# Expert-choice routing behind a GRU: the search for each expert's last weight, by 17 bits and MAX8 instead of 30 bits and a stage for ties

## The chip, the core and the metric

The kernel runs on one core of a Trainium2 chip. The metric is device time in microseconds; before the change the median of three runs is 1204.65 us (1203.07 to 1211.93). A profile of one execution stands beside it. The names of the engines in it: PE is TensorE (PEld its weight loads), DVE VectorE, ACT ScalarE, POOL GpSimd, SP SyncE, which issues most of the transfers.

## What is computed

A GRU runs over 256 steps for 16 sequences of width 512. Its states are 4096 tokens. A router gives each token a softmax over 16 experts, and every expert chooses the k = 256 tokens that have the largest weights for it (expert choice). All experts share one matrix, so a token's result is its expert output times the sum of the weights with which it was chosen.

```python
def cell(h, x):                       # scanned over 256 steps
    gi = x @ W_ih + b_ih
    gh = h @ W_hh + b_hh
    r = sigmoid(i_r + h_r); z = sigmoid(i_z + h_z)
    n = tanh(i_n + r * h_n)
    return (1.0 - z) * n + z * h

logits = xf @ router_w + router_b     # xf: the 4096 states
S = softmax(logits, axis=-1)
G, idx = top_k(S.T, 256)              # each of 16 experts takes 256 tokens
out = einsum('ekh,hd->ekd', xf[idx], expert_w) + expert_b
y = zeros.at[idx].add(G[..., None] * out)
return x + y
```

Top-k takes the earlier token where weights are equal. So a kernel that finds the k-th largest weight of each expert, and keeps all weights at or above it, agrees with the reference as long as exactly 256 weights are kept; where several weights equal the k-th, it also has to rank them.

## The kernel before

The 256 steps are cut into 32 groups of 8 steps; a group is 128 tokens (16 sequences x 8 steps) and fills the partitions. The recurrence (all lines up to 538) takes most of the time and is the same in both kernels. Between its steps TensorE also makes the expert product of the states for 15 of the groups. The other 17 are "late groups" (line 124: the odd ones and the last but one): their expert product is made after the recurrence, by a generator that is called wherever TensorE would stand idle. `late_part` (line 132) is the smallest piece of it, a part: four matmuls with 256 columns each, side by side in four column strips. Eight parts are a group, so there are 136 parts. `expert_for(n)` (line 181) emits the next n parts at this place of TensorE's order.

A late group is summed in a PSUM bank. There are five banks for it (`ps_m` two, `ps_e` three). `late_begin` (line 153) writes the bias into a bank with ScalarE; it is emitted in the middle of the group two before it and has to wait until the bank's former content is used. As long as the gates are not known, a finished group is copied to SBUF by ScalarE (line 175). Once they are known (`gated`), it stays in its bank and the last step reads it there (line 172).

The routing stage (lines 566 to 678) has TensorE, ScalarE and VectorE in the order in which the code is written. The 4096 weights of an expert are laid out as 8 partitions of 512 elements (`sT`, by four transposes). A positive float32 orders like its bit pattern, so the k-th largest weight is found bit by bit, from bit 29 down to 0 (line 599): VectorE compares all weights with a candidate and counts per partition (line 602), TensorE adds the counts of an expert's eight partitions with the 0/1 matrix `same_h` (line 607), and two tiny VectorE steps (610 and 613) keep or drop the bit. Behind each count's matmul stand two late parts, or three where the bit is odd (line 608). The result `kth` is exact.

Then comes the stage for equal weights (lines 623 to 657): where a weight equals `kth`, its rank among its equals is found by a scan in a partition and two matmuls across partitions (641, 642), and compared with the room that is left below 256 (648 to 652). Ten late parts stand beside it. Kept weights are multiplied out in four pieces (660), each followed by a matmul (663) that sums a token's weights over the experts into `pg`. That becomes `gate` (665).

In the last step (670 to 678) VectorE makes for each group `xs = sums * gate + xs` (673) and SyncE stores the group, 256 KB each (676). The 15 groups of the recurrence come first, then the late groups as they finish: TensorE's remaining parts are emitted one by one in line 672 until the next late group is done.

Of the kernel before, what the change touches and what calls it, by code (L numbers as in the profile page):

```python
# [8 lines left out]
F32 = mybir.dt.float32  # L9
BF16 = mybir.dt.bfloat16  # L10
F16 = mybir.dt.float16
I32 = mybir.dt.int32
AF = mybir.ActivationFunctionType
ALU = mybir.AluOpType
AX = mybir.AxisListType
# [3 lines left out]
def kernel(  # L19
# [34 lines left out]
    nc = tc.nc  # L54
    B, T, D = x.shape
    E = router_w.shape[1]
    P = 128
    QD = 32
    KC = D // P
    TG = P // B  # L60
    NG = T // TG
    TOPK = min(B * T // E, B * T)
# [3 lines left out]
    xs = const.tile([P, NG, D], F32, name="xs")  # L66
# [4 lines left out]
    lg = const.tile([P, E, NG], F32, name="lg")  # L71
    eb = const.tile([P, D], F32, name="eb")
# [4 lines left out]
    QG = NG * E // P  # L77
    GH = P // E
# [31 lines left out]
    def begin_sums(bank):  # L110

        n = bank.shape[-1]
        for j in range(KC):
            nc.tensor.matmul(
                bank[QD * j : QD * (j + 1)],
                zero,
                zero[:, 0:E].unsqueeze(1).to_broadcast([P, n // E, E]),
                start=True,
                stop=True,
                tile_position=(0, QD * j),  # L120
            )
# [4 lines left out]
    def wide(g):  # L126

        return ht[:, g, :, :].rearrange("p k d -> p (k d)")
# [3 lines left out]
    def late_part(g, pe, part):  # L132

        k, h = divmod(part, 2)
        cols = slice(HD * h, HD * (h + 1))
        for j in range(KC):
            q = slice(QD * j, QD * (j + 1))
            nc.tensor.matmul(  # L138
                pe[q, cols],
                ht[:, g, k, q],  # L140
                ewr[:, k, E:][:, cols],
                start=False,
                stop=(k == KC - 1),
                tile_position=(0, QD * j),
                skip_group_check=True,
            )

    late = []
    late_sums = {}
# [31 lines left out]
    def expert_for(n):  # L181
        for _ in range(n):
            next(parts, None)
# [382 lines left out]
    with (  # L566
        tc.tile_pool(name="route", bufs=1) as rt,
        tc.tile_pool(name="work", bufs=2) as wk,
        tc.tile_pool(name="ps_s", bufs=1, space=bass.MemoryType.PSUM) as ps_s,
        tc.tile_pool(name="ps_c", bufs=1, space=bass.MemoryType.PSUM) as ps_c,  # L570
        tc.tile_pool(name="ps_n", bufs=1, space=bass.MemoryType.PSUM) as ps_n,
        tc.tile_pool(name="ps_e", bufs=3, space=bass.MemoryType.PSUM) as ps_e,
        tc.manual_schedule(engines={mybir.EngineType.PE, mybir.EngineType.Activation, mybir.EngineType.DVE}),
    ):
        late_pool.append(ps_e)
        keep = rt.tile([P, B, QG * TG], F32, name="keep")
        nc.gpsimd.memset(keep, 1.0)
        nc.gpsimd.memset(keep[:, :, 0:1], 0.0)

        ps = ps_s.tile([P, QG, P], F32, name="ps", tag="s")  # L580
        ps_last = ps_n.tile([P, P], F32, name="ps_last", tag="n")
        lg_f = lg.rearrange("p e g -> p (e g)")
        sT = rt.tile([P, QG * P], F32, name="sT")
        for q in range(QG - 1):
            nc.tensor.transpose(ps[:, q, :], lg_f[:, q :: QG], ident)
        nc.tensor.transpose(ps_last, lg_f[:, QG - 1 :: QG], ident)
        by_row = lambda ap: ap.rearrange("p (q b t) -> p b q t", q=QG, b=B)
        by_step = lambda ap: ap.rearrange("p b (q t) -> p b q t", q=QG)
        nc.scalar.copy(sT[:, 0 : (QG - 1) * P], ps[:, 0 : QG - 1, :].rearrange("p q n -> p (q n)"))
        nc.vector.tensor_copy(sT[:, (QG - 1) * P :], ps_last)  # L590

        HIGH = 29
        cand = wk.tile([P, 1], I32, name="cand")
        nc.vector.memset(cand, 1 << HIGH)
        ge = rt.tile([P, QG * P], BF16, name="ge")
        counts = ps_c.tile([P, HIGH + 1], F32, name="counts")
        for bit in range(HIGH, -1, -1):
            cnt = wk.tile([P, 1], F16, name="cnt")  # L600
            with nc.allow_low_precision("whole numbers up to a row's length, exact in float16"):
                nc.vector.tensor_scalar(
                    ge, sT, cand.bitcast(F32), None, ALU.is_ge, ALU.add, accum_out=cnt
                )

            n = counts[:, bit : bit + 1]
            nc.tensor.matmul(n, same_h, cnt, start=True, stop=True)
            expert_for(2 + bit % 2)
            off = wk.tile([P, 1], I32, name="off")
            nc.vector.tensor_scalar(off, n, float(TOPK), float(1 << bit), ALU.is_lt, ALU.mult)  # L610
            nxt = wk.tile([P, 1], I32, name="cand")
            if bit:
                nc.vector.scalar_tensor_tensor(
                    nxt, cand, 1 << (bit - 1), off, ALU.bitwise_or, ALU.bitwise_xor
                )
            else:
                nc.vector.tensor_tensor(nxt, cand, off, ALU.bitwise_xor)
            cand = nxt
        kth = cand.bitcast(F32)

        eq = rt.tile([P, B, QG * TG], F32, name="eq")
        nc.vector.tensor_scalar(by_step(eq), by_row(sT), kth, None, ALU.is_equal)
        rank = rt.tile([P, B, QG * TG], F32, name="rank")
        nc.vector.tensor_tensor_scan(
            rank.rearrange("p b t -> p (b t)"),
            keep.rearrange("p b t -> p (b t)"),
            eq.rearrange("p b t -> p (b t)"),
            0.0,  # L630
            ALU.mult,
            ALU.add,
        )
        row = rt.tile([P, B], F32, name="row")
        nc.vector.tensor_scalar(row, rank[:, :, QG * TG - 1], -1.0, None, ALU.mult)
        upto = rt.tile([P, B], F32, name="upto")
        nc.vector.tensor_tensor_scan(upto, ones_b, row, 0.0, ALU.mult, ALU.add)
        nc.vector.tensor_tensor(upto, upto, row, ALU.subtract)
        expert_for(4)
        n_first = ps_n.tile([P, B], F32, name="n_first", tag="n")  # L640
        nc.tensor.matmul(n_first, before_f, row, start=True, stop=False)
        nc.tensor.matmul(n_first, same_f, upto, start=False, stop=True)
        expert_for(6)
        at_least = rt.tile([P, QG * P], F32, name="at_least")
        nc.vector.scalar_tensor_tensor(at_least, sT, kth, sT, ALU.is_ge, ALU.mult)
        nc.vector.tensor_tensor(rank, rank, eq, ALU.mult)
        too_few = rt.tile([P, HIGH + 1], F32, name="too_few")
        nc.vector.tensor_copy(too_few, counts)
        nc.vector.scalar_tensor_tensor(too_few, too_few, float(TOPK), too_few, ALU.is_lt, ALU.mult)
        room = rt.tile([P, 1], F32, name="room")  # L650
        nc.vector.tensor_reduce(room, too_few, AX.X, ALU.max)
        nc.vector.tensor_scalar(room, room, -1.0, float(TOPK), ALU.mult, ALU.add)
        last = rt.tile([P, B], F32, name="last")
        nc.vector.tensor_scalar(last, n_first, room, 0.0, ALU.add, ALU.max)
        nc.vector.tensor_tensor(
            rank, rank, last.unsqueeze(2).to_broadcast([P, B, QG * TG]), ALU.is_le
        )
        pg = ps_s.tile([P, QG, GH], F32, name="pg", tag="s")
        for q in range(QG):
            nc.vector.tensor_tensor(  # L660
                by_row(at_least)[:, :, q, :], by_step(rank)[:, :, q, :], by_row(at_least)[:, :, q, :], ALU.mult
            )
            nc.tensor.matmul(pg[:, q, :], at_least[:, q * P : (q + 1) * P], row_of, start=True, stop=True)
        gate = rt.tile([P, NG], F32, name="gate")
        nc.vector.tensor_copy(
            gate.rearrange("p (h q) -> p h q", q=QG), pg.rearrange("p q h -> p h q")
        )

        gated.append(True)
        for g in [g for g in range(NG) if g not in late_groups] + late_groups:  # L670
            while g in late_groups and g not in late_done:
                expert_for(1)
            nc.vector.scalar_tensor_tensor(  # L673
                xs[:, g, :], late_sums.get(g, wide(g)), gate[:, g : g + 1], xs[:, g, :], ALU.mult, ALU.add
            )
            nc.sync.dma_start(
                out=out[:, g * TG : (g + 1) * TG, :], in_=xs[:, g, :]
            )


# [29 lines left out]
```

## Time and profile before

| | us |
|---|---|
| median of three runs | 1204.65 (1203.07 to 1211.93) |
| the profiled execution: its time | 1206.33 |
| the profiled execution: its span, first to last instruction | 1204.3 |
| TensorE busy | 1162.3 (97%) |
| TensorE weight loads busy | 1048.4 (87%) |
| VectorE busy | 699.2 (58%) |
| ScalarE busy | 323.3 (27%) |
| mean granted TensorE clock | 0.995 |
| first transpose of the routing stage ends, about | 1120 |
| first compare of the search | 1120.77 |
| the last candidate, line 617 | 1166.61 |
| first add of the last step | 1174.03 |
| last add starts | 1198.15 |

The span is the time between the first and the last instruction of the profiled execution; 2.0 us of that execution's time lie around it. A row of instructions in order of time gives start, duration, engine, line, operation, output and inputs, shapes and how many were merged; in brackets stands how long the engine was idle before it and what ended that wait. A matmul in float32 leaves two records for each instruction. Where a row says "issue", the profile shows nothing that the engine waited for.

### The profile page before, as it was taken

Reading aid. Unit: us, or ns where it says so; the run is one execution under the profiler, and the core shown is the slowest. Engines: PE = TensorE matmul, PEld = TensorE weight load, DVE = VectorE, ACT = ScalarE, POOL = GpSimd, SP = SyncE. Lnnn points to the kernel's source line nnn. Section 1 sums busy time; section 2 is a strip of 40 time slices with the busy share of each in tenths; the row PEclk is TensorE's granted clock in tenths of the full one; section 3 lists DMA queues with packets and bytes.
Section 4 is the critical chain, followed back from the end, with each engine's and each line's share of the span. In section 5 each row is a group of like instructions: output and inputs, shape, how many; then the busy total and the mean of one; then the engine's idle time right before and its main releaser. Section 6 shows DMA issues by size and latency. Waiting matters only on the chain. (4 is left out here: it accounts for less than half of the span.)

```text
span 1204.3 us, 80850 instructions
## 1 busy us (share of the span) xinstructions
PE 1162.3 (97%) x36490; PEld 1048.4 (87%) x36490; DVE 699.2 (58%) x3919; ACT 323.3 (27%) x1435; POOL 100.2 (8%) x406
## 2 busy tenths in 40 slices
PE   5999999999999999999999999999999999999897
PEld 3899999999999988999999999999889999998444
DVE  2555655565555555555565556565555555565777
ACT  0223222222222222222222222222222222222220
POOL 3000000000000000000000000000000000000000
PEclk9999999999999999999999999999999999999998
DMA  8000000000000000000000000000000000000008
GB/s 273 23 22 20 20 20 20 19 20 20 20 22 20 20 18 19 20 19 20 22 19 20 17 22 20 20 20 20 19 20 20 20 20 20 22 9 13 2 2 280
DMA packets 48345, 38.05 MB, mean 32 GB/s; under 512 B 7744, under 2 KB 40064, under 8 KB 48000
## 3 DMA queue, kind: packets, MB, share of 16 engines
q1 hardware_dynamic: 45856, 29.43, 8.4%
q8 instruction: 286, 4.69, 1.6%
q10 hardware_dynamic: 1632, 3.15, 0.8%
q14 instruction: 59, 0.48, 0.1%
q0 software_dynamic: 512, 0.31, 0.1%
HBM read 24.47 MB, written 8.39 MB: 27 GB/s over the span
## 5 line engine op out<-in xcount | busy, mean ns | idle before, releaser
L411 PE MATMUL ra<-whh,hs 128*16 128x128 f32 (+1 forms) x8192 | 345.6, 273 | 7.6 <-DVE zT L497 5.2
L411 PE MATMUL hn<-whh,hs 128*16 128x128 f32 (+1 forms) x8192 | 345.4, 273 | 0.0
L485 DVE TENSOR_TENSOR t<-r,hn 128x64 f32<-128x64 f32 x512 | 90.2, 217 | 364.1 <-PE hn L411 360.6
L398 PE MATMUL ra<-wih,xt 128*32 128x256 f32 x4096 | 288.0, 382 | 7.6 <-DVE xt L253 6.0
L411 PE MATMUL zz<-whh,hs 128*16 128x128 f32 (+1 forms) x8192 | 287.8, 273 | 2.6 <-issue 2.4
L411 PEld LDWEIGHTS ra<-whh,hs 128*16 128x16 f32 (+1 forms) x8192 | 243.3, 103 | 16.8 <-issue 6.8
L411 PEld LDWEIGHTS hn<-whh,hs 128*16 128x16 f32 (+1 forms) x8192 | 256.8, 103 | 0.4 <-issue 0.2
L411 PEld LDWEIGHTS zz<-whh,hs 128*16 128x16 f32 (+1 forms) x8192 | 239.6, 103 | 6.2 <-issue 5.5
L468 ACT ACTIVATE r<-ra 128x128 f32<-128x128 f32 x256 | 71.1, 278 | 598.4 <-PE ra L411 598.4
L398 PEld LDWEIGHTS ra<-wih,xt 128*32 128x32 f32 x4096 | 156.6, 111 | 43.2 <-issue 8.3
L489 ACT ACTIVATE n<-t 128x64 f32<-128x64 f32 x512 | 103.4, 248 | 192.8 <-DVE t L487 192.5
L398 PE MATMUL zz<-wih,xt 128*32 128x128 f32 x4096 | 147.1, 273 | 1.5 <-issue 1.2
L398 PEld LDWEIGHTS zz<-wih,xt 128*32 128x32 f32 x4096 | 128.9, 110 | 17.2 <-issue 4.1
L494 DVE STREAM_TRANSPOSE nT<-n 128x64 f32<-128x64 f32 x512 | 100.6, 234 | 57.3 <-ACT n L489 57.0
L497 DVE STREAM_TRANSPOSE zT<-zs 128x64 f32<-128x64 f32 x512 | 121.8, 238 | 3.7 <-ACT zs L490 3.1
L508 DVE TENSOR_TENSOR hs<-v,nT 128x32 f32<-128x32 f32 x512 | 101.7, 199 | 21.7
L505 DVE TENSOR_TENSOR v<-u,zT 128x32 f32<-128x32 f32 x512 | 104.3, 204 | 8.8
L365 PE MATMUL pe<-ewr,ht 128*32 128x136 f32 (+1 forms) x1920 | 107.6, 276 | 0.0
L487 DVE TENSOR_TENSOR t<-t,ra 128x64 f32<-128x64 f32 x512 | 88.2, 213 | 0.1
L365 PEld LDWEIGHTS pe<-ewr,ht 128*32 128x32 f32 x1920 | 75.0, 110 | 11.8 <-issue 0.2
L500 DVE TENSOR_TENSOR u<-hs,nT 128x32 f32<-128x32 f32 x512 | 78.2, 153 | 0.0
L138 PE MATMUL pe<-ewr,ht 128*32 128x256 f32 x1088 | 69.4, 395 | 1.9 <-ACT pe L158 1.9
(108 smaller groups left out, 518.8 us busy)
## 6 DMA issues: line engine op xcount, KB each, us to landing
xs<-in_x_dram SPq DMA_DIRECT2D x128, 64.0 KB, 2.3
out_dram<-xs SPq DMA_DIRECT2D x32, 256.0 KB, 4.0
xa<-in_x_dram SPq DMA_DIRECT2D x248, 32.0 KB, 2.1
wih<-in_L_cond_W_ih_dram ACTq DMA_DIRECT2D x3, 512.0 KB, 8.9
wih<-in_L_cond_W_ih_dram SPq DMA_DIRECT2D x3, 512.0 KB, 7.9
whh<-in_L_cond_W_hh_dram SPq DMA_DIRECT2D x3, 512.0 KB, 14.1
whh<-in_L_cond_W_hh_dram ACTq DMA_DIRECT2D x3, 512.0 KB, 14.6
ewr<-in_L_ffn_expert_w_dram SPq DMA_DIRECT2D x1, 1024.0 KB, 5.9
```

Of the source, the lines that this page charges most:

```text
L365: nc.tensor.matmul(pe[quadrant(j), at : at + w], ht[:, g, k, quadrant(j)], ewr[:, k, src : src + w], start=(k == 0), stop=(k == KC - 1), t ...
L398: nc.tensor.matmul(dst, lhs, rhs, start=False, stop=(k == KC - 1), tile_position=(0, QD * j), skip_group_check=True)
L411: nc.tensor.matmul(dst[quadrant(j, m)], lhs, columns(whh[:, k, gate_, :], j), start=False, stop=(k == KC - 1), tile_position=(0, QD * j), ...
L468: nc.scalar.activation(r, ra[p % 2][:, 0, :], AF.Sigmoid)
L485: nc.vector.tensor_tensor(t[half], r[:, cols], hn[p % 2][:, cols], ALU.mult)
L487: nc.vector.tensor_tensor(t[half], t[half], ra[p % 2][:, 1, cols], ALU.add)
L489: nc.scalar.activation(n[half], t[half], AF.Tanh)
L494: nc.vector.transpose(nT[half], n[half])
L497: nc.vector.transpose(zT[half], zs[:, halves[half][1]])
L500: nc.vector.tensor_tensor(u[half], hs[:, halves[half][2], slot(s), :], of_step(nT[half], odd), ALU.subtract)
L505: nc.vector.tensor_tensor(v[half], u[half], of_step(zT[half], odd), ALU.mult)
L508: nc.vector.tensor_tensor(hs[:, halves[half][2], slot(s + 1), :], v[half], of_step(nT[half], odd), ALU.add)
```

## The change

Four things change, all in the routing stage and behind it.

1. The search runs over the bits 27 to 11 alone, 17 instead of 30. The bits 29 and 28 are taken as given (`KNOWN`, weights from 2^-31 to just under 2), and the 11 low bits are left open: the result is a bracket, of which `top` is the upper end.
2. Within the bracket the k-th weight is chosen with MAX8, VectorE's operation that gives the eight largest elements of each partition. Weights above the bracket are set to zero, MAX8 takes the eight largest of each of an expert's eight partitions, a float32 matmul with `same_f` brings these 64 to all eight partitions, and MAX8 takes the eight largest of them. The number of weights above the bracket (`above`, from the counts of the search) says which of the eight is the k-th. Four late parts stand in this stage, two on each side of the matmul.
3. There is no stage for equal weights any more in the main path: weights at or above `kth` are kept.
4. Behind the third add a check is made: the weights at or above `kth` are counted once more, and where an expert's count isn't 256, a flag is set. At the end of the program each engine reads the flag; where it is set, x is loaded again and the whole routing is done over, with all 30 bits and the stage for equal weights, and all groups are stored again. SyncE and GpSimd are not under the written order; on SyncE the read of the flag comes to stand behind the third of the 32 stores.

The lists of TensorE, ScalarE and VectorE stand in the written order up to the flag; within the branch they don't.

```diff
-        HIGH = 29
-        cand = wk.tile([P, 1], I32, name="cand")
-        nc.vector.memset(cand, 1 << HIGH)
-        counts = ps_c.tile([P, HIGH + 1], F32, name="counts")
-        for bit in range(HIGH, -1, -1):
...
-            expert_for(2 + bit % 2)
...
-        eq = rt.tile([P, B, QG * TG], F32, name="eq")
-        nc.vector.tensor_scalar(by_step(eq), by_row(sT), kth, None, ALU.is_equal)
...
+        def count(at, name):
+            cnt = wk.tile([P, 1], F16, name=name)
...
+                nc.vector.tensor_scalar(
+                    ge, sT, at.bitcast(F32), None, ALU.is_ge, ALU.add, accum_out=cnt
+                )
+            return cnt
+
+        def by_bits(known, high, low, counts, meanwhile):
+            below = (1 << low) - 1
+            cand = wk.tile([P, 1], I32, name="cand")
+            nc.vector.memset(cand, known | 1 << high)
+            for bit in range(high, low - 1, -1):
+                cnt = count(cand, "cnt")
+                n = counts[:, bit - low : bit - low + 1]
+                nc.tensor.matmul(n, same_h, cnt, start=True, stop=True)
+                meanwhile(bit)
+                off = wk.tile([P, 1], I32, name="off")
+                nc.vector.tensor_scalar(off, n, float(TOPK), float(1 << bit), ALU.is_lt, ALU.mult)
...
+        def above(counts):
+            n = counts.shape[-1]
+            too_few = rt.tile([P, n], F32, name="too_few")
+            nc.vector.tensor_copy(too_few, counts)
+            nc.vector.scalar_tensor_tensor(too_few, too_few, float(TOPK), too_few, ALU.is_lt, ALU.mult)
+            room = rt.tile([P, 1], F32, name="room")
+            nc.vector.tensor_reduce(room, too_few, AX.X, ALU.max)
+            nc.vector.tensor_scalar(room, room, -1.0, float(TOPK), ALU.mult, ALU.add)
+            return room
...
+        HIGH, LOW, KNOWN = 27, 11, 3 << 28
+        NTOP = 8
+        flag = rt.tile([1, 1], I32, name="flag")
+        order = rt.tile([P, NTOP], F32, name="order")
+        for i in range(NTOP):
+            nc.gpsimd.memset(order[:, i : i + 1], float(i + 1))
...
+            counts = ps_c.tile([P, HIGH - LOW + 1], F32, name="counts")
+            top = by_bits(KNOWN, HIGH, LOW, counts, lambda bit: expert_for(2 + bit % 2))
+            nc.vector.scalar_tensor_tensor(at_least, sT, top.bitcast(F32), sT, ALU.is_le, ALU.mult)
+            most = rt.tile([P, NTOP], F32, name="most")
+            nc.vector.max(out=most, in_=at_least)
+            spread = rt.tile([P, GH, NTOP], F32, name="spread")
+            nc.vector.tensor_tensor(
+                spread,
+                row_of.unsqueeze(2).to_broadcast([P, GH, NTOP]),
+                most.unsqueeze(1).to_broadcast([P, GH, NTOP]),
+                ALU.mult,
+            )
+            expert_for(2)
+            all_most = ps_n.tile([P, GH * NTOP], F32, name="all_most", tag="n")
+            nc.tensor.matmul(all_most, same_f, spread.rearrange("p h n -> p (h n)"), start=True, stop=True)
+            expert_for(2)
+            room = above(counts)
+            nc.vector.max(out=most, in_=all_most)
+            kth = rt.tile([P, 1], F32, name="kth")
+            nc.vector.scalar_tensor_tensor(
+                order, order, room, most, ALU.is_equal, ALU.mult, accum_out=kth
+            )
+            pg = ps_s.tile([P, QG, GH], F32, name="pg", tag="s")
+            for q in range(QG):
+                part = slice(q * P, (q + 1) * P)
+                nc.vector.scalar_tensor_tensor(at_least[:, part], sT[:, part], kth, sT[:, part], ALU.is_ge, ALU.mult)
+                sum_weights(q, pg)
+            gate = gate_of(pg)
+
+            gated.append(True)
+            for i, g in enumerate([g for g in range(NG) if g not in late_groups] + late_groups):
+                while g in late_groups and g not in late_done:
+                    expert_for(1)
+                store(g, late_sums.get(g, wide(g)), gate)
+                if i == 2:
+                    n = ps_n.tile([P, 1], F32, name="n", tag="n")
+                    nc.tensor.matmul(n, same_h, count(kth, "cnt"), start=True, stop=True)
+                    wrong = wk.tile([P, 1], F16, name="wrong")
+                    nc.vector.tensor_scalar(wrong, n, float(TOPK), None, ALU.not_equal)
+                    n_wrong = ps_n.tile([1, 1], F32, name="n_wrong", tag="n")
+                    nc.tensor.matmul(n_wrong, wrong, wrong, start=True, stop=True)
+                    nc.vector.tensor_copy(flag, n_wrong)
+
+        again = nc.values_load(flag, min_val=0, max_val=P)
+        with tc.If(again > 0):
+            keep = rt.tile([P, B, QG * TG], F32, name="keep")
...
+            for g in range(NG):
+                nc.sync.dma_start(out=xs[:, g, :], in_=x[:, g * TG : (g + 1) * TG, :])
+            counts = ps_c.tile([P, 30], F32, name="counts")
+            kth = by_bits(0, 29, 0, counts, lambda bit: None).bitcast(F32)
...
```

`sum_weights`, `gate_of` and `store` hold the matmul of line 663, the copy of line 665 and the add with its store (673, 676) as they were.

## The prediction

> **What bounds the kernel now.** I read the page first (TensorE busy 97% of the span; the recurrence fills the first 1119 us and the change does not touch it), then the instructions in order of time from 1119 us to the end, engine by engine, then the clock and the transfer rate in stretches of the tail. The chain of waits that the page prints ends at the last residual add and shows only "issue" before it, so the chain is followed by hand.
>
> The search first, two bits of it on VectorE:
>
> ```profile
> 1162.32 0.75 DVE L602 TENSOR_SCALAR_CACHE_REDUCE ge<-sT,cand 128x512 bf16<-128x512 f32 x1
> 1162.99 0.09 DVE L602 DVE_READ_ACCUMULATOR ge<-sT,cand 128x1 f16 x1
> 1163.48 0.16 DVE L610 TENSOR_SCALAR off<-counts 128x1 int32<-128x1 f32 x1 [0.40 <-PE counts L607]
> 1163.67 0.16 DVE L613 SCALAR_TENSOR_TENSOR cand<-cand,off 128x1 int32<-128x1 int32 x1
> 1163.87 0.75 DVE L602 TENSOR_SCALAR_CACHE_REDUCE ge<-sT,cand 128x512 bf16<-128x512 f32 x1
> 1164.54 0.09 DVE L602 DVE_READ_ACCUMULATOR ge<-sT,cand 128x1 f16 x1
> 1164.88 0.16 DVE L610 TENSOR_SCALAR off<-counts 128x1 int32<-128x1 f32 x1 [0.25 <-PE counts L607]
> ```
>
> A bit is a serial loop: compare and count, matmul, two tiny VectorE steps. From 1162.32 to 1163.87 it takes 1.55 us, the next one (to 1165.27) 1.40: the long one follows an odd bit, behind whose count TensorE has three parts of the late expert matmuls (one call of `late_part` is one part; there are 17 groups x 8 = 136), the short one an even bit with two. So VectorE's chain sets the pace while TensorE fills it with late parts. Now the tail on TensorE:
>
> ```profile
> 1169.64 2.80 PE L138 MATMUL pe<-ewr,ht 128*32 128x256 f32 x48
> 1172.71 1.06 PE L663 MATMUL pg<-row_of,at_least 128*128 128x8 f32 x8 [0.27 <-DVE at_least L660]
> 1173.69 17.04 PE L138 MATMUL pe<-ewr,ht 128*32 128x256 f32 x312
> 1192.68 5.35 PE L138 MATMUL pe<-ewr,ht 128*32 128x256 f32 x64 [1.95 <-ACT pe L158]
> ```
>
> and on VectorE:
>
> ```profile
> 1174.03 17.32 DVE L673 SCALAR_TENSOR_TENSOR xs<-ht,gate,xs 128x512 f32<-128x512 f32 x26
> 1191.27 3.38 DVE L673 SCALAR_TENSOR_TENSOR xs<-pe,gate,xs 128x512 f32<-128x512 f32 x5
> 1198.15 0.75 DVE L673 SCALAR_TENSOR_TENSOR xs<-pe,gate,xs 128x512 f32<-128x512 f32 x1 [3.51 <-issue]
> ```
>
> A part is 8 records. 312 records, 39 parts, take 17.04 us: 0.437 us each. The 3.51 us marked "issue" are really a wait for TensorE: the last add starts 0.12 us after the last matmul ends at 1198.03. That matmul's group was late because its PSUM bank was freed only by an add (ScalarE's copy of the bias at 1192.04 waited 17.8 us for it), and then because the clock fell. The stretches of the tail:
>
> ```profile
> 1174.00:1190.70 16.70, 16.70 (x312) 9.82 (x304) 16.67 (x26) 0.27 (x1) 0.00 (x0) 1.00 0.85 272
> 1190.70:1192.60 1.90, 0.04 (x4) 0.00 (x0) 1.90 (x4) 0.56 (x1) 0.00 (x0) 1.00 1.01 323
> ...
> 1193.40:1196.70 3.30, 3.30 (x36) 1.69 (x32) 1.24 (x2) 0.00 (x0) 0.00 (x0) 0.50 1.02 345
> ...
> 1198.10:1202.20 4.10, 0.00 (x0) 0.00 (x0) 0.75 (x1) 0.00 (x0) 0.00 (x0) 0.75 0.97 337
> 1202.20:1204.30 2.10, 0.00 (x0) 0.00 (x0) 0.00 (x0) 0.00 (x0) 0.00 (x0) 0.50 0.03 13
> ```
>
> Columns: stretch, length, busy time of TensorE, weight loads, VectorE, ScalarE, GpSimd, then granted clock, share of the DMA engines, GB/s. After a gap of 1.9 us TensorE ran at half clock for 3.3 us, which made the last eight parts 5.35 us instead of 3.5. The stores saturate the DMA engines at some 340 GB/s until 1202.2, and 2.1 us of closing follow. So at the end three things finish almost together: late matmuls, adds, stores. The late matmuls are work that was put into the search's gaps; the point of the whole sum is where they go when the search shrinks.
>
> **The change, part by part.**
>
> *Thirteen bits fewer (30 to 17).* Six of those are odd, seven even, counting alike at both ends: 6 x 1.54 + 7 x 1.40 = 19.0 us of VectorE's chain. With them go 6 x 3 + 7 x 2 = 32 parts that TensorE did meanwhile.
>
> *The stage for equal weights.* From the last candidate (1166.77) to the first add (1174.03) it takes 7.26 us now. In its place, serially: masking 512 weights, 0.67 (pitch of L645); MAX8 over 512; an outer product, 0.22 (128x64 multiply of the recurrence, 217 ns); a matmul, 0.4 (L641); then max over 64 and the choice by rank, 0.5 from small rows of 0.18 to 0.23 with the accumulator read; four masked multiplies at 0.25 (L660's pitch is 0.22); and pg, gate and first add 0.8 as now. MAX8 is not in the trace: bounds 0.49 (L624, one pass over 512) and 1.23 (L626, a scan); I take 0.68, the L646 pass. TensorE reaches the new matmul about 0.4 late, since three parts of the last bit and two more stand ahead. The count-to-room steps lie beside it. Sum 5.1, so 2.2 us less. It also carries 4 parts where there were 10: 6 more are moved.
>
> The gate is thus ready at 1174.03 - 19.0 - 2.2 = 1152.8.
>
> *What is late next.* Behind the gate stood 47 parts; now 47 + 32 + 6 = 85, or 37.1 us of TensorE where 20.5 were. Of the 21.2 us won, 16.6 come back. VectorE (32 adds at 0.664, 21.2 us) and the stores are faster than that, so TensorE sets the end. No bank stall remains: parts for the five banks last 16 us from TensorE's restart, and VectorE frees the first bank 15.9 us after the gate.
>
> *The check of the count.* Placed after the third add, it stands in TensorE's order between pg and all 85 parts. Who waits: those parts. Today TensorE resumes 0.35 us ahead of the first add. Now: three adds 2.0, count and matmul to VectorE's next step 1.01 (1160.92 to 1161.93, a bit), its comparison 0.16, the second matmul 0.35: it resumes 3.5 us after the gate, at 1156.3. On VectorE 29 adds are queued behind it, with slack.
>
> *The clock after that gap.* TensorE stands for some 4.3 us. The row above shows half clock for 3.3 us after 1.9 us of standing, worth 1.85. [...] by the row it costs about 1.85. [...] taken 2.0.
>
> *SyncE.* In the changed order the read of the flag stands behind the third store and ahead of the other 29, so these wait for VectorE's flag, some 4 us after the gate, plus the read. At 0.77 us a store (256 KB at 340 GB/s) they need 22.3 us and are through about 1181, long before TensorE: nothing, with TensorE as its cover.
>
> *The branch.* Each engine reads the flag and jumps over some 150 instructions (VectorE) at its end. No row shows a register load or jump. [...] A transfer's nearest row is 2.1 us to landing (xa loads). [...] Both lie partly beside the last store, which lands 2.9 us after it is issued. [...] taken 1.0, near the low end for that cover. The memsets of `order` and the flag reads on ScalarE and GpSimd hold nothing up.
>
> **The sum.** 1156.3 + 37.1 + 2.0 = 1195.4 for the last late matmul (1198.03 now); 0.12 + 0.75 for its add; 0.4 to its issue, 2.9 to land, 2.1 closing, 1.0 for the branch: 1202.7 against a span of 1204.3, a gain of 1.6. The profiled execution took 1206.33 (2.0 around its span) and the median is 1204.65 (1203.07 to 1211.93); less 1.6, about 1203.0. About 1% is what a measurement of this kernel can tell from no change.
>
> **The rivals.**
>
> *The search's time is simply won* (0.05). If late parts were free, the stores would bound: 29 of them from about 1159, 22.3 us, closing: near 1184. For it: the adds and stores alone fit. Against it: TensorE is busy 16.70 of 16.70 us behind the gate already.
>
> *The check and the branch eat the gain* (0.18): [...]: 1207. For it: the clock row; against: the last store's landing covers most.
>
> *The branch is taken* (0.05), the slower side. It is decided by one thing, whether the fp32 matmul hands the chosen weight on bit for bit; rounded up in one expert of 16, that count is 255, not 256. Then 30 bits without cover (30 x 1.40 = 42), the old stage (7.3) and all adds and stores from the gate to the end (30.3) follow the last add at some 1196 plus 3: 1279 span, 1280. [...] Ties and more than eight in the bracket are far off: 2048 float steps hold one weight per expert when the reference's softmax is computed and counted.
>
> **How the numbers follow.** Forecast 0.72, check and branch 0.18, gain won 0.05, branch taken 0.05. Faster by over 1% needs the second bound to fall: 0.05; slower by over 1%: 0.05; within 1%: 0.90. Range: low with no clock loss, no branch cost and 1 us less in the new stage, 1199; high with the second rival's ends, 1207.5.
>
> **What would show it.** Right: 340 late matmuls (680 records) in one block after the gate with a gap of about 4 us ahead and half clock at its start, the gate near 1153, adds from PSUM 3.5 us apart at the end, DMA engines no longer full at the end. Wrong: a TensorE gap among the late groups, a part off 0.437 us, a second search in the trace, or more than 5 us between the last store's landing and the end.

## The result, and the profile after

The changed kernel takes 1201.68 us (median of 20 runs, 1195.9 to 1206.91) against 1206.98 us of the kernel before (20 runs, 1202.59 to 1211.93). The ratio is 0.9958, 95% interval 0.9944 to 0.9972: by it 5.1 us faster, with 3.4 to 6.8 in the interval. That is within 1%, and the time lies inside the range. The forecast gain was 1.6 us, some 3.5 short; where these lie is worked out below.

The profiled execution has a span of 1199.3 us. Its instructions in order of time, on TensorE, behind the search:

```profile
1149.80 1.18 PE L628 MATMUL pg<-row_of,at_least 128*128 128x8 f32 x8
1154.04 0.16 PE L702 MATMUL n<-cnt,same_h 128*128 128x1 f16 x1 [3.06 <-DVE ge L585]
1154.46 0.16 PE L706 MATMUL n_wrong<-wrong 128*1 128x1 f16 x1 [0.25 <-DVE wrong L704]
1154.47 39.05 PE L138 MATMUL pe<-ewr,ht 128*32 128x256 f32 x680
```

All 85 late parts (680 records) stand in one block behind the check, as the written order says, and the block is now the tail: before, it was 47 parts in two pieces. TensorE stood for 3.06 us because the check's first matmul waits for VectorE's count; from the end of pg's matmuls to the block it is 3.5 us.

The same on VectorE, from the last step of the search:

```profile
1146.24 0.16 DVE L608 SCALAR_TENSOR_TENSOR cand<-cand,off 128x1 int32<-128x1 int32 x1
1146.43 0.75 DVE L667 SCALAR_TENSOR_TENSOR at_least<-sT,cand 128x512 f32<-128x512 f32 x1
1147.22 0.69 DVE L669 MAX8 most<-at_least 128x8 f32<-128x512 f32 x1
...
1148.78 0.22 DVE L682 MAX8 most<-all_most 128x8 f32<-128x64 f32 x1
...
1151.24 2.08 DVE L638 SCALAR_TENSOR_TENSOR xs<-ht,gate,xs 128x512 f32<-128x512 f32 x3
1153.23 0.74 DVE L585 TENSOR_SCALAR_CACHE_REDUCE ge<-sT,kth 128x512 bf16<-128x512 f32 x1
...
1154.74 12.00 DVE L638 SCALAR_TENSOR_TENSOR xs<-ht,gate,xs 128x512 f32<-128x512 f32 x18
...
1190.20 0.75 DVE L638 SCALAR_TENSOR_TENSOR xs<-pe,gate,xs 128x512 f32<-128x512 f32 x1 [2.69 <-PE pe L138]
1193.65 0.75 DVE L638 SCALAR_TENSOR_TENSOR xs<-pe,gate,xs 128x512 f32<-128x512 f32 x1 [2.70 <-DMA out_dram<-xs]
```

The first add starts at 1151.24 instead of 1174.03. But the last adds stand 3.45 us apart, eight parts each, and VectorE idles 2.7 us before each of them. (The last row names a DMA as the releaser; that add starts 0.13 us after the last matmul, like its predecessors.) So 22.8 us won at the gate have become 4.5 us at the last add (1194.40 is its end, 1198.90 before); 1.2 us of either lie ahead of the search's fourth count, as the next section says.

The stretches of the tail, with the columns as before (after the engines: granted clock, share of the DMA engines, GB/s):

```profile
1151.20:1154.40 3.20, 0.16 (x1) 0.00 (x0) 2.91 (x7) 0.00 (x0) 0.00 (x0) 0.63 0.33 90
1154.40:1158.00 3.60, 3.54 (x37) 1.66 (x41) 3.34 (x7) 0.00 (x0) 0.00 (x0) 0.50 0.62 192
1158.00:1162.00 4.00, 4.00 (x72) 2.10 (x68) 4.00 (x7) 0.00 (x0) 0.00 (x0) 0.89 0.95 301
1162.00:1180.00 18.00, 18.00 (x341) 9.79 (x336) 9.12 (x15) 3.54 (x6) 0.00 (x0) 1.00 0.85 276
1180.00:1193.60 13.60, 13.51 (x252) 7.13 (x244) 2.86 (x4) 0.00 (x0) 0.00 (x0) 1.00 0.29 78
```

The clock falls to half in the gap and stays there for the first 4.4 us of the block. At the end the DMA engines are busy 0.29 of the time; before, 0.97 to 1.02 of it from 1190.7 up to 1202.2.

### The profile page after: what moved, and what is told of

Its sections match the earlier page's. It is cut to its first block, busy times and chain, and to the rows that moved or that the text cites. A ratio compares the mean times of both kernels' runs of the same rounds, so it can differ in the third digit from the quotient of the medians.

```text
span 1199.3 us, 80820 instructions
## 1 busy us (share of the span) xinstructions
PE 1158.5 (97%) x36477; PEld 1050.0 (88%) x36477; DVE 685.8 (57%) x3868; ACT 320.5 (27%) x1430; POOL 99.5 (8%) x412
## 4 chain that ended last, share of the span: by engine, by line
PE 91%; DVE 5%; DMA 1%; issue 1%; ACT 1%; POOL 0%; DVEq 0%; ACTq 0%; POOLq 0%
PE ra L411 19%; PE hn L411 19%; PE ra L398 17%; PE zz L411 17%; PE zz L398 10%; PE pe L365 5%; PE pe L138 4%; DVE nT L494 1%; DVE t L485 1%; DVE zT L497 1%; ACT n L489 1%; DMA xs<-in_L_cond_b_hh_dram 1%; DVE ge L585 1%; DMA xs<-in_cond_dram 0%; DVE hs L508 0%
```

## The experiments

To compare tails I measure from the fourth count of the search, here before and after:

```profile
1127.76 0.18 PE L607 MATMUL counts<-cnt,same_h 128*128 128x1 f16 x1
```

```profile
1126.56 0.18 PE L600 MATMUL counts<-cnt,same_h 128*128 128x1 f16 x1
```

Everything ahead of it is the same work, and its time varies by itself: from profile to profile the fourth count starts anywhere from 1121.6 (e9) to 1128.6 us (e2). From there to the end the kernel before takes 76.5 us and the changed one 72.7, 3.8 less; the other 1.2 us between the two spans lie ahead of that point and are not the change's.

**No check, no branch (e1).** The theory was that late matmuls set the end, and that the check costs the gap and the clock. The edit takes out the check, the flag and the whole branch.

```diff
-                if i == 2:
-                    n = ps_n.tile([P, 1], F32, name="n", tag="n")
...
-                    nc.vector.tensor_copy(flag, n_wrong)
-        again = nc.values_load(flag, min_val=0, max_val=P)
-        with tc.If(again > 0):
...
```

> The changed kernel without the check behind the third add, without the flag and without the branch (the repeat for failed counts is left out, so ties would not be handled; the rest is computed). Theory, TensorE's late matmuls set the end: they start about 0.3 us ahead of the first add instead of 3.2 us behind it, and the block of 85 parts takes 37.1 us instead of 39.05, since no gap throttles the clock; the last late matmul comes 5.5 us earlier and the ratio to the kernel before is near 0.991. Rival, VectorE's adds or the stores set the end: only the 1.4 us of VectorE's check can go, ratio 0.995 or above. Rival, the branch costs the end a microsecond or more: the last add moves by 5.5 us and the span by 6.5 or more.

Ratio 0.991 (0.9896 to 0.9924). TensorE in order of time:

```profile
1150.04 1.18 PE L628 MATMUL pg<-row_of,at_least 128*128 128x8 f32 x8
1151.15 36.90 PE L138 MATMUL pe<-ewr,ht 128*32 128x256 f32 x680
```

The block starts 0.33 us ahead of the first add (1151.48), and its 85 parts take 36.90 us, 2.15 less than behind the gap. From the fourth count it starts 3.6 us earlier than in the changed kernel. With 1.0 us less at the end the tail is 66.0 us, 6.8 shorter. The last add comes as the theory said; the microsecond at the end belongs to the second rival, and e5 asks for it.

**The check later in TensorE's order (e2).** All of the changed kernel is kept.

```diff
                 if i == 2:
-                    n = ps_n.tile([P, 1], F32, name="n", tag="n")
-                    nc.tensor.matmul(n, same_h, count(kth, "cnt"), start=True, stop=True)
+                    cnt = count(kth, "cnt")
+                    expert_for(8)
+                    n = ps_n.tile([P, 1], F32, name="n", tag="n")
+                    nc.tensor.matmul(n, same_h, cnt, start=True, stop=True)
+                if i == 8:
                     wrong = wk.tile([P, 1], F16, name="wrong")
                     nc.vector.tensor_scalar(wrong, n, float(TOPK), None, ALU.not_equal)
+                    expert_for(12)
                     n_wrong = ps_n.tile([1, 1], F32, name="n_wrong", tag="n")
                     nc.tensor.matmul(n_wrong, wrong, wrong, start=True, stop=True)
+                if i == 20:
                     nc.vector.tensor_copy(flag, n_wrong)
```

> All of the changed kernel, but the check's first matmul stands behind the first 8 of the 85 late parts and its second behind 12 more, with VectorE's steps at the ninth and the 21st add, so that TensorE never waits for the check. Theory: as without the check, last late matmul some 5 us earlier, ratio near 0.9915; the branch stays, hidden beside the last store. Rival, the branch or the flag is what costs: no gain over the changed kernel, ratio 0.995 to 0.996.

Ratio 0.9931 (0.9918 to 0.9945), a smaller gain than expected. TensorE in order of time:

```profile
1152.90 3.66 PE L138 MATMUL pe<-ewr,ht 128*32 128x256 f32 x64
1156.49 0.18 PE L703 MATMUL n<-cnt,same_h 128*128 128x1 f16 x1
1156.60 5.39 PE L138 MATMUL pe<-ewr,ht 128*32 128x256 f32 x96
1161.80 0.17 PE L709 MATMUL n_wrong<-wrong 128*1 128x1 f16 x1
1161.81 28.52 PE L138 MATMUL pe<-ewr,ht 128*32 128x256 f32 x520
```

The tail is 67.6 us, 5.2 shorter than the changed kernel's. Of this 3.6 come from the earlier start and 1.6 from the late parts themselves: at full clock throughout (1.00 from 1153 to 1190), with the check's two matmuls among them, they end 37.4 us after their start. So the place of the check in TensorE's order carried 5.2 of the 6.8 us; branch and flag are still there, and the span ends 4.9 us behind the last add as in the changed kernel.

**Seventeen bits alone (e3).** Change 1 without changes 2 to 4.

```diff
-        HIGH = 29
+        HIGH, LOW, KNOWN = 27, 11, 3 << 28
...
-        nc.vector.memset(cand, 1 << HIGH)
+        nc.vector.memset(cand, KNOWN | 1 << HIGH)
...
-        for bit in range(HIGH, -1, -1):
+        for bit in range(HIGH, LOW - 1, -1):
```

> The kernel before with the search cut to the bits 27 to 11 and nothing else: stage for equal weights as before, no MAX8, no check, no branch. The chosen threshold is the lower end of the bracket, so weights inside the bracket below the 256th would be kept too. Theory: gate near 1153.7, 79 parts of 0.437 us behind it (34.5), last late matmul near 1188, about 5.5 us earlier than in the changed kernel, ratio near 0.991: the MAX8 stage itself is worth about nothing, since it saves 2.2 us and moves six parts (2.6 us) behind the gate. Rival, the search's time is simply won: 19 us, ratio 0.984. Rival, the stage for equal weights was the costly part: no better than the kernel before by more than 2 us.

Ratio 0.9899 (0.988 to 0.9918). TensorE:

```profile
1151.29 1.06 PE L663 MATMUL pg<-row_of,at_least 128*128 128x8 f32 x8
1152.28 34.31 PE L138 MATMUL pe<-ewr,ht 128*32 128x256 f32 x632
```

632 records are the expected 79 parts. The gate comes 2.5 us later than in the changed kernel (27.1 against 24.7 from the fourth count), and the tail is still 65.8 us, no longer than without any check at all. So the MAX8 stage and the dropped tie stage are worth nothing for the time here; they are worth exactness, since a 17-bit threshold alone keeps the whole bracket. The search's 19 us show up as about 11: the 32 parts that come back cost 13.8, and the wait for a bank, the half clock and the queue of stores at the end of the kernel before are gone, as the account behind the experiments shows.

**Dummy work in the gap (e4).**

```diff
+                    junk = ps_n.tile([P, D], F32, name="junk", tag="n")
+                    for _ in range(7):
+                        begin_sums(junk)
                     n = ps_n.tile([P, 1], F32, name="n", tag="n")
```

> The changed kernel with 28 matmuls of zeros into the check's PSUM bank between pg and the check (some 2.8 us of TensorE work that nothing uses), so that TensorE waits for nothing long, while the late parts start at the same time as in the changed kernel. Theory, half clock after the gap costs 1.9 us by itself: clock 1.0 through the tail, block of 85 parts 37.1 us, ratio near 0.994. Rival, the half clock is hidden because the parts wait for banks or copies anyway: block and time as in the changed kernel, ratio 0.9958.

Ratio 0.9946 (0.9931 to 0.9961). The interval overlaps that of the changed kernel, so the time alone does not decide; the trace does:

```profile
1149.74 1.71 PE L114 MATMUL junk<-zero 128*32 128x512 bf16 x28
1152.87 0.18 PE L705 MATMUL n<-cnt,same_h 128*128 128x1 f16 x1 [1.43 <-DVE ge L585]
1153.30 0.16 PE L709 MATMUL n_wrong<-wrong 128*1 128x1 f16 x1 [0.25 <-DVE wrong L707]
1153.31 36.89 PE L138 MATMUL pe<-ewr,ht 128*32 128x256 f32 x680
```

The dummy matmuls take 1.71 us, less than was planned, and TensorE still waits 1.43 us for the check. The parts start 27.9 us after the fourth count, as in the changed kernel, and the block takes 36.89 us, as without the check. The clock is 1.00 from the gap to the end of the block, and over the whole span it is 0.998 in each of the six runs, against 0.994 to 0.997 in the twenty of the changed kernel. In these two profiles the half clock by itself costs 2.16 us, and nothing else moved: the tail is 70.6 us, 2.15 shorter.

**Check and flag without the branch (e5).**

```diff
-        again = nc.values_load(flag, min_val=0, max_val=P)
-        with tc.If(again > 0):
...
```

> The changed kernel with the check and the flag, but without reading the flag and without the branch (the repeat for failed counts is left out). In the changed kernel and in the two runs that keep the branch the span ends 4.9 us after the last add, in the two without it 3.9. Theory, the flag's read and the branch cost 1.0 us at the end and nothing else: last add to end 3.9 us, ratio near 0.995. Rival, they cost nothing and the shorter end belongs to something else of those two runs: 4.9 us, ratio as of the changed kernel, 0.9958.

Ratio 0.995 (0.993 to 0.9969). This interval too holds the changed kernel's 0.9958, so again the trace decides. The last add starts at 1194.40, ends 0.75 later, and the span is 1199.0: 3.85 us to the end, as expected. The branch in the changed kernel, by engine (count, then shortest/median/longest duration in ns, then the start of the first and the last):

```profile
L710 SPq EVENT_SEMAPHORE  x8: 17/17/17, 1195.5 to 1197.6; - x8
...
L710 PEldq COMPARE_BRANCH  x1: 3592/3592/3592, 1193.2 to 1193.2; - x1
L710 DVEq COMPARE_BRANCH  x1: 76/76/76, 1194.8 to 1194.8; - x1
L710 SPq COMPARE_BRANCH  x1: 45/45/45, 1195.0 to 1195.0; - x1
```

The last store and SyncE's closing, in the changed kernel and then in e1, which has no branch:

```profile
L641 SPq DMA_DIRECT2D out_dram<-xs x32: 537/571/1432, 1152.0 to 1194.4; - x32
L789 SPq DRAIN  x3: 7/7/13, 1198.4 to 1198.8; - x3
```

```profile
L641 SPq DMA_DIRECT2D out_dram<-xs x32: 538/620/1948, 1152.3 to 1188.9; - x32
L726 SPq DRAIN  x3: 7/7/129, 1191.8 to 1192.4; - x3
```

The jump takes 45 to 76 ns on SyncE and VectorE, and 3.6 us on TensorE, whose jump is over at 1196.8. SyncE is the later one: behind its jump it waits for eight semaphores, by their times those of the stores, until 1197.6, and then goes through its closing list of waits until 1198.4. From the last store's issue to that point it takes 4.0 us here and 2.9 without the branch (e1, and 1187.5 to 1190.4 in e3). So the microsecond is SyncE's, and TensorE's 3.6 us lie beside the last store's landing.

**Three late parts behind every count (e6)**, on top of the late check.

```diff
-            top = by_bits(KNOWN, HIGH, LOW, counts, lambda bit: expert_for(2 + bit % 2))
+            top = by_bits(KNOWN, HIGH, LOW, counts, lambda bit: expert_for(3))
```

> The kernel with the late check, with three late parts behind every count instead of two or three. Theory, TensorE's work is only shifted and its gaps are what counts: the eight even bits take 1.54 us instead of 1.40, so the gate comes 1.1 us later, but 8 parts (3.5 us) less stand behind it: 2.4 us faster than the late check, ratio near 0.991. Rival, the search's length on VectorE is what counts: 1.1 us slower, ratio 0.994.

Ratio 0.9904 (0.9883 to 0.9925). The gate comes later and the end earlier:

```profile
1161.25 7.53 PE L138 MATMUL pe<-ewr,ht 128*32 128x256 f32 x136
1169.52 17.47 PE L138 MATMUL pe<-ewr,ht 128*32 128x256 f32 x320 [0.74 <-ACT pe L158]
```

The late matmuls are through at 1186.99. From the first count of the search, with the late parts behind it at the same pace in both (16 records in 1.05 us), it takes 70.8 us to the end, 1.4 less than with the late check alone (72.2); 2.4 were expected, and 0.74 of the difference is the wait for a bank in the second row. By the ratios this is the fastest of the kernels that do all of the work, clear of the kernel before and of the changed one; its interval still meets that of the late check alone.

**Three late parts in the kernel before (e7).** The same idea where the gate, not TensorE, should be the later one.

```diff
-            expert_for(2 + bit % 2)
+            expert_for(3)
```

> The kernel before with three late parts behind each of its 30 counts, nothing else changed. The gate comes 15 x 0.14 = 2.1 us later, and 15 parts (6.6 us) less stand behind it. Theory: with so few parts left (32, 14 us), the stores set the end; they need 27.4 us from the first issue and are 2.1 us later, so the kernel is some 2 us slower, ratio 1.001 to 1.002. Rival, TensorE alone sets the end of the kernel before: 4.5 us faster or more, ratio 0.996 or less.

Ratio 1.0013 (0.9999 to 1.0027). The rival's 0.996 is ruled out and the theory's 1.001 to 1.002 fits; that the kernel is slower at all is not shown. TensorE first, then VectorE:

```profile
1175.85 14.02 PE L138 MATMUL pe<-ewr,ht 128*32 128x256 f32 x256
```

```profile
1176.18 18.64 DVE L673 SCALAR_TENSOR_TENSOR xs<-ht,gate,xs 128x512 f32<-128x512 f32 x28
1194.74 2.72 DVE L673 SCALAR_TENSOR_TENSOR xs<-pe,gate,xs 128x512 f32<-128x512 f32 x4
```

TensorE is through at 1189.9, more than 15 us before the span's end at 1205.6. From the gate to the end it takes 29.4 us, and the kernel before took 30.3. TensorE is done 13.7 us behind the gate instead of 24.0, and the end comes only 0.9 us nearer to it. SyncE issues the 32 stores over 24.8 us, from 1176.96 to 1201.79; an estimate from the tail before, 0.77 us a store, gives 24.6. So in the kernel before the stores hang on the gate, and TensorE's end is near the same time: both chains have to get shorter. The change shortens the one by 22 us and leaves the other as the bound.

**The branch taken (e8).**

```diff
-                    nc.vector.tensor_scalar(wrong, n, float(TOPK), None, ALU.not_equal)
+                    nc.vector.tensor_scalar(wrong, n, float(TOPK), None, ALU.is_equal)
```

> The changed kernel with the check's comparison turned round, so that the flag is set where the counts are right and the branch is taken: the routing is done twice and everything is stored twice. The prediction priced this at 1280 us, +75: 42 for 30 bits without cover, 7.3 for the old stage, 30.3 from the gate to the end and 3 for flag and branch. Rival, the repeat isn't in a written order and has no work beside it[...]: 1290 or more; or its adds and late matmuls lie beside the search: 1265 or less.

1295.03 us, ratio 1.0743 (1.0717 to 1.0769), 90 us and not 75. VectorE:

```profile
1195.11 0.74 DVE L585 TENSOR_SCALAR_CACHE_REDUCE ge<-sT,cand 128x512 bf16<-128x512 f32 x1
...
1237.65 0.16 DVE L606 TENSOR_TENSOR cand<-cand,off 128x1 int32<-128x1 int32 x1
...
1245.41 8.70 DVE L638 SCALAR_TENSOR_TENSOR xs<-ht,gate,xs 128x512 f32<-128x512 f32 x13
...
1267.09 0.75 DVE L638 SCALAR_TENSOR_TENSOR xs<-pe,gate,xs 128x512 f32<-128x512 f32 x1 [3.67 <-PE pe L138]
...
1291.21 0.75 DVE L638 SCALAR_TENSOR_TENSOR xs<-pe,gate,xs 128x512 f32<-128x512 f32 x1 [3.81 <-PE pe L138]
```

The second search takes 42.7 us (42 were priced) and the old stage 7.6 (7.3), but from the gate to the end it takes 50.4, not 30.3. The adds from PSUM wait for TensorE again: a part of the late groups is made ahead of the gate, until 1217.5, and the others from 1256.2 on, where TensorE's last long wait (9.68 us) ends with an add. TensorE's jump takes 0.19 us here at most, where the repeat is entered and not skipped.

**No late parts behind the gate (e9).**

```diff
-                late_part(g, pe, part)
+                if not gated:
+                    late_part(g, pe, part)
```

> The changed kernel without the 85 late parts behind the gate (the expert product of 11 late groups is left out, wholly or in part; banks, copies, adds, check, stores and branch stay). It asks what the search's time would be worth if TensorE had no late work. Theory and the prediction's first rival agree on what is left, the stores: 29 of them from about 1156 at 0.77 us are through near 1178 to 1180, and with landing, branch and closing the span ends at 1181 to 1184, ratio near 0.982 to 0.985. If it ends above 1190, something other than late matmuls and stores bounds the tail.

Ratio 0.9843 (0.9812 to 0.9874), in the expected place. The last adds on VectorE, and stretches with the columns as before:

```profile
1161.69 7.32 DVE L639 SCALAR_TENSOR_TENSOR xs<-pe,gate,xs 128x512 f32<-128x512 f32 x11
```

```profile
1160.00:1165.00 5.00, 0.00 (x0) 0.00 (x0) 5.00 (x9) 2.33 (x4) 0.00 (x0) 0.50 0.98 326
1170.00:1174.00 4.00, 0.00 (x0) 0.00 (x0) 0.00 (x0) 0.00 (x0) 0.00 (x0) 0.50 1.01 345
```

The adds are through at 1169.0, the DMA engines are busy 0.98 to 1.01 from 1160 to 1176, and the span ends at 1178.9. This is the first rival's price with its obstacle taken away: without the late matmuls the change would be worth some 1.6%, and the stores would be the bound.

## Why the prediction was right, and where it was off

The accounts of the two profiles from the fourth count on, in us:

| | predicted | measured |
|---|---|---|
| the gate comes earlier | 21.2 | 21.6 |
| of this: thirteen bits | 19.0 | 19.2 |
| of this: MAX8 in place of the tie stage | 2.2 | 2.4 |
| from the gate to the last add's end, before 24.9 | 43.5 | 43.2 |
| of this: TensorE resumes behind the gate | 3.5 | 3.2 |
| of this: 85 parts, half clock with them | 37.1 + 2.0 | 39.05 |
| from the last add's end to the end of the span, before 5.4 | 6.4 | 4.9 |
| the tail in all | -1.6 | -3.8 |

The gain that is left is a balance of its own. Of the 21.6 us at the gate, 38 more parts at full clock take back 16.4, the later start of the block 3.6 and its half clock 2.15. In return the kernel before had 1.95 us of waiting for a bank and 1.85 of half clock in its tail, which are gone, and its end was 0.5 longer. Together that is the 3.8.

**The search's time comes back.** Right, with its size: 38 parts of 0.437 us reappear behind the gate, and TensorE sets the end. Right too that no wait for a bank remains: the block stands in one piece. e3 shows it for the bits alone, e9 shows what they would be worth without the parts, and e7 shows the other half, that the kernel before hung on the gate as well.

**MAX8.** The value taken between 0.49 and 1.23 was 0.68 us; it takes 0.69 over 512 elements and 0.22 over 64 from PSUM. The sum of that stage has a slip: the terms listed add up to 4.7 us, not 5.1. From the last candidate to the first add the changed kernel takes 4.84, so either figure was near.

**The check in front of 85 parts.** Right: the place costs 3.6 us against a resumption 0.3 us ahead of the gate (e1, e2), and the clock 2.15 more (e4). The 2.0 was the author's estimate; the row of the 1.9 us gap (1.85) was near it. But 2.15 is one draw: behind the same wait e5's block takes 38.58 us, only 1.7 more than e4's. That the 2.0 came so near is in part luck. TensorE stood 3.5 us, not the 4.3 that the prediction gave; its own terms make 3.8.

**The flag ahead of 29 stores.** Right: on SyncE the stores wait, and nothing follows from it, since TensorE is later.

**The end.** This is the term that was mis-sized, in the step "0.4 to its issue, 2.9 to land, 2.1 closing, 1.0 for the branch". The 1.0 for the branch measured 1.0 (e5), but that is luck: it was the author's estimate of the part of a jump that the last store doesn't cover, with no row of a jump behind it, while TensorE's long jump (3.6 us) is covered whole and what the end does pay for is SyncE's additional waits. The other three were read from the kernel before, where a queue of stores stood ahead of the last one. In the kernels without branch that pace their last stores by TensorE, the last add's end is followed by the end of the span after 3.8 to 3.9 us (e1, e3, e5) instead of 5.4; from the last store's issue to SyncE's first drain it takes 2.9 us in e1 and e3 and 4.1 in the kernel before. The prediction named a likely reason among its signs ("DMA engines no longer full at the end") and did not put it into the sum: 1.5 us too much. No run changes the queue of stores alone.

**The rivals.** The gain is not simply won (e9 shows the condition). That check and branch eat the gain was right in kind (without them the ratio is 0.991 instead of 0.9958) and wrong in size. Its 1207, and with it the upper end of the range, was the author's estimate. The half clock did last 6.8 us, but 2.4 of them fell into the gap, where they cost nothing; and a long jump, 3.6 us, is TensorE's alone, and is hidden. That the branch is taken did not occur: the profile has no second search, so every expert's count was 256 with the weight that the fp32 matmul handed on. That an fp32 matmul hands a weight on bit for bit was the author's estimate: the times show only what the type costs. In e4 a set of four strips of 512 bfloat16 columns takes 0.40 us alone and seven sets 1.71, so one more is 0.22 us, against 0.437 for four strips of 256 float32 columns: a float32 column takes four times as long. The price of a taken branch was 15 us too low (e8), in the step "all adds and stores from the gate to the end (30.3)", which left out that the late matmuls would follow the gate there too.

**The rest of the measured gain.** The ratio says 5.1 us with 3.4 to 6.8 around it, the tails say 3.8. These agree within the interval. The 1.2 us that the profiles differ by ahead of the fourth count is small beside the 7 us that this point moves from profile to profile. The runs also tell more than the prediction's "about 1%": a ratio of 1 lies outside their interval.

## What to carry to other kernels

Work that was put into the gaps of a serial loop doesn't vanish when the loop gets shorter: count it out, add it behind, and see which chain is then last. In a kernel where two chains end together, shorten both or expect the smaller part of the gain. A test that nothing needs soon can stand anywhere in the order of an engine that is full, and the place where that engine has to wait for it is the dear one: with 8 and 20 late parts ahead of its two matmuls (e2) the check for which TensorE had waited 3.06 us made it wait for nothing.

## What the runs showed of the hardware that was not expected

**Behind the same short gap the clock was half in one execution and full in another.** Ahead of the search TensorE waits 1.3 us for the first count, in a thinly filled stretch (it is busy for 0.70 of the 2 us from 1119 to 1121 in the changed kernel, and for 0.87 from 1121 to 1123 in e1). The instructions are the same in the changed kernel and in e1. The first count of the changed kernel (its fourth, at 1126.56, is shown above), and the first and the fourth of e1:

```profile
1120.59 0.16 PE L600 MATMUL counts<-cnt,same_h 128*128 128x1 f16 x1 [1.30 <-DVE ge L585]
```

```profile
1122.13 0.16 PE L600 MATMUL counts<-cnt,same_h 128*128 128x1 f16 x1 [1.29 <-DVE ge L585]
...
1126.82 0.18 PE L600 MATMUL counts<-cnt,same_h 128*128 128x1 f16 x1
```

From the first count to the fourth it takes 6.19 us in the kernel before, 5.97 in the changed one and 5.98 in e3, with 3.4 us of half clock in it each time, and 6.18 in e5, where 16 late records take 1.94 us there and 1.07 later; but 4.69 in e1, e2, e4 and e9, at full clock (1.00 in the stretches of e1, e2 and e4; in e9 16 late records take 1.04 us). In e2 and e4 the half clock came earlier and ended some 2 us ahead of the first count; in e1 the clock is 1.00 from 1117 on.

**The clock was half, and full, for multiples of 3.41 us.** In the changed kernel's profile the granted clock is half from 1121.33 to 1124.75 us (3.41 us), full for 27.31 (eight times that), half from 1152.05 to 1158.88 (6.83, twice) and full for 37.55 (eleven times). In the kernel before it is half from 1121.66 to 1125.08, full for 68.27 (twenty times) and half from 1193.34 to 1196.76. In these two profiles each stretch between two changes is a whole multiple of 3.41 us. Two of the changed kernel's edges, by the column of the granted clock (the third from the end):

```profile
1152.00:1152.40 0.40, 0.00 (x0) 0.00 (x0) 0.40 (x1) 0.00 (x0) 0.00 (x0) 0.57 0.00 0
...
1158.80:1159.20 0.40, 0.40 (x12) 0.24 (x8) 0.40 (x1) 0.00 (x0) 0.00 (x0) 0.90 1.02 343
```

In the changed kernel's check the clock was halved at 1152.05, 1.1 us after the last matmul before it; in the 3.41 us ahead of that edge TensorE had been busy for 2.21. What decides when it is halved is not shown. Nor did the same wait cost the same: behind the check's 3.06 us the clock was half for 6.83 us in the changed kernel's profile, while e5's block is 1.7 us longer than e4's at full clock (38.58 against 36.89), by estimate the price of 3.4 us of half clock. Half clock behind the first count is worth 1.3 to 1.5 us of the stretch to the fourth (5.97 to 6.19 against 4.69), so two profiles should be compared from a point behind it.

**Skipping the branch was long on one engine only.** It took TensorE 3.4 to 3.9 us (3.59 in the changed kernel, 3.35 in e2, 3.91 in e4), the other engines 0.045 to 0.076. What fills this time is not shown. Reading the flag took 0.47 to 0.59 us on each engine in the changed kernel. Whether TensorE's jump would show if nothing lay beside it was not tried.
